# Block 0's y in three float32r passes, a one-operation mask, and a full-tile count, in the head of an attention and FFN layer

## The chip, the cores and the metric

One core of a Trainium2 chip runs the whole layer. The metric is the device time of one execution in microseconds (us). Engines: PE is TensorE (matmuls; PEld are its weight loads), DVE is VectorE, ACT is ScalarE, POOL is GpSimd, SP is SyncE, which issues most DMAs.

## The reference

Tokens x are (4, 2048, 256), taken as 8192 rows of 256 features. A first part is attention inside chunks of 32 tokens, a second part a feed-forward network with integer weights; each adds its input and ends in a layer norm.

```
Q, K, V = x @ W_q.T, x @ W_k.T, x @ W_v.T
mask[i, j] = decay ** (i - j) if i >= j else 0      # decay = sigmoid(log_decay[0]), 32 x 32
S = (Qc @ Kc.T) * mask                              # in each chunk of 32 tokens
O = S @ Vc
out = (sigmoid(x @ W_g.T) * O) @ W_o.T + x
x = layernorm(x + out)
h = silu(x @ (w_gate/127).T) * (x @ (w_up/127).T)   # 768 hidden features
x = layernorm(x + h @ (w_down/127).T)
```

## The kernel before

The tokens go in 16 blocks of 512 (TB). Everything is written out by hand, block by block; `in_turn` keeps the order of the written lines on each engine. While the FFN of block b runs, the attention of the next blocks runs between its pieces. The head, before that steady order, has to bring in and prepare the weights and to do the attention of blocks 0 and 1; it is what the change rearranges.

**Scores without Q and K.** The head makes m from W_q and W_k once (`make_m`, L220). For a block, y is m applied to x (feature-major, 256 x 512), and the scores are products of x and y in 32 x 32 pieces (`score_products`, L663, PE tiles of 128 x 32). `masked` (L679) multiplies the scores by the mask into sT on DVE. sT pairs two chunks: a row of 128 tokens has 64 columns, of which its own chunk's 32 are written; the other 32 stay zero from a memset at the start. `masked` therefore does four operations, one for each chunk of 32 partitions. `value_products` (L699, PE tiles of 64 x 64) multiplies sT and v into two PSUM banks po; L718 multiplies po by the gate into goT on DVE, for block 0 in four halves (`by_half`); `attn_residual` (L811) multiplies goT by W_o for block 0, the tile pa; L802 adds x and makes h.

**Two ways to multiply.** Block 0's gate (`attn_gate`, L587), value (`attn_v`, L629), y (`attn_y`, L608) and output (L811) are plain float32 matmuls; the profile shows each as two passes. All later blocks use `three` (L542): both operands are split into float32r parts and multiplied in three passes, high x high, low x low, gap x gap. Between the second and the third, ACT multiplies the PSUM bank by a constant (L542). `others()` runs the third pass later; the code calls it `g_rest`, `v_rest`, `y_rest` or `rest`.

**Making the parts.** Weights: `weight_parts` makes hi on ACT (L448) and lo on POOL (L449), `weight_up` scales lo on ACT (L455), `weight_gap` makes gap on POOL (L461). Tokens: hi on ACT (L472), lo on POOL (L476), gap on DVE (L481). Each is one operation of 128x512, two of them for a block's tokens.

**The order in the head** (L1078 on). Weight parts of wg; mask (`make_mask`, DVE); gate of block 0; hi and lo of block 1's tokens; value of block 0 with m made between its halves; y of block 0; gaps of wg and wv; parts of wo; gaps of block 1's tokens; gate and value of block 1 (first two passes); scores of block 0, then the load of block 2's xT, which takes the buffer of block 0's; rests of gate and value 1; y of block 1 (first two passes); values of block 0 (po); rest of y 1; output of block 0 (pa) with the scores of block 1 behind it; then block 2's value, and so on. `look_up` (L295, DVE) finds the largest integer of each FFN weight piece, `cast_...` (L286, ACT) turn the integers into the two FFN weight types. Whether any integer is too large is counted by a matmul of a [128, 1] tile of ones with a [128, 9] tile (`count_wide`, L313, the tile pw).

Of the kernel before, what the change touches and what calls it, by code (L numbers as in the profile page):

```python
# [47 lines left out]
F32 = mybir.dt.float32  # L48
# [4 lines left out]
ALU = mybir.AluOpType  # L53

P = 128
CHUNK = 32
PAIR = 2 * CHUNK
# [19 lines left out]
def kernel(  # L77
# [37 lines left out]
    def in_turn(ins):  # L115
        tc.keep_in_program_order(ins)

    def bank(name):
        return psum.tile([P, TB], F32, tag="ps", name=name)
# [119 lines left out]
        )  # L239
    chunk_mask = const.tile([P, CHUNK], F32, tag="chunk_mask", name="chunk_mask")  # L240
    nc.vector.tensor_scalar(chunk_mask, diff, 0.0, None, ALU.is_ge)
    table = tiny.tile([P, 1], F32, tag="table", name="table")
    in_turn(nc.scalar.activation(table, eps, AF.Sigmoid))
    bits = []
# [14 lines left out]
    def make_mask():  # L259
        in_turn(nc.scalar.activation(decay, decay, AF.Sigmoid))  # L260
        power = decay
        for i, (bit, factor) in enumerate(bits):
            in_turn(
                nc.vector.scalar_tensor_tensor(factor, bit, power, factor, ALU.mult, ALU.add)
            )
            in_turn(nc.vector.tensor_tensor(chunk_mask, chunk_mask, factor, ALU.mult))
            if i < len(bits) - 1:
                square = tiny.tile([P, 1], F32, tag=f"power_{i}", name=f"power_{i}")
                in_turn(nc.vector.tensor_tensor(square, power, power, ALU.mult))
                power = square  # L270

    sTs = [const.tile([P, NG, PAIR], F32, tag=f"sT_{i}", name=f"sT_{i}") for i in range(2)]
    for sT in sTs:
        nc.gpsimd.memset(sT, 0.0)

    def integers(w, w_int, name):

# [26 lines left out]
    def wide_counter():  # L304

        wide = const.tile([P, top.shape[1]], F32, tag="wide", name="wide")
        in_turn(nc.vector.tensor_scalar(wide, top, EXACT, None, ALU.is_gt))
        ones = tiny.tile([P, 1], F32, tag="ones", name="ones")
        nc.vector.memset(ones, 1.0)

        def count_wide():
            pw = bank("pw")[:1, : top.shape[1]]
            in_turn(nc.tensor.matmul(pw, lhsT=ones, rhs=wide, start=True, stop=True))  # L313
            count = tiny.tile([1, 1], F32, tag="count", name="count")
            in_turn(nc.vector.tensor_reduce(count, pw, mybir.AxisListType.X, ALU.add))
            return count

        return count_wide
# [123 lines left out]
    def weight_parts(w, name, tags):  # L442

        hi, lo = (
            const.tile([P, KD, D], F32R, tag=tag, name=f"{name}_{kind}")
            for tag, kind in zip(tags, ("hi", "lo"))
        )
        in_turn(nc.scalar.mul(hi, w, TOP))  # L448
        in_turn(nc.gpsimd.tensor_tensor(lo, w, hi.bitcast(F32), ALU.subtract))  # L449
        w_parts[name] = [hi, lo]  # L450

    def weight_up(name):

        lo = w_parts[name][1]
        in_turn(nc.scalar.mul(lo, lo.bitcast(F32), SHIFT))  # L455

    def weight_gap(name):

        hi, lo = w_parts[name]
        gap = const.tile([P, KD, D], F32R, tag=name, name=f"{name}_gap")  # L460
        in_turn(nc.gpsimd.tensor_tensor(gap, hi.bitcast(F32), lo.bitcast(F32), ALU.subtract))  # L461
        w_parts[name].append(gap)

    def pieces_of_tokens(t, name):

        hi, lo, gap = parts = [
            sums.tile([P, KD, TB], F32R, tag=f"{name[0]}_{kind}", name=f"{name}_{kind}")
            for kind in ("hi", "lo", "gap")
        ]

        def high(k):
            in_turn(nc.scalar.mul(hi[:, k, :], t[:, k, :], TOP))  # L472

        def low(k):
            whole = hi[:, k, :].bitcast(F32)
            in_turn(nc.gpsimd.tensor_tensor(lo[:, k, :], t[:, k, :], whole, ALU.subtract))  # L476

        def difference(k):
            whole = hi[:, k, :].bitcast(F32)
            in_turn(  # L480
                nc.vector.scalar_tensor_tensor(  # L481
                    gap[:, k, :], whole, -WHOLE, t[:, k, :], ALU.mult, ALU.add
                )
            )

        return parts, high, low, difference

    def token_parts(t, name):
        parts, high, low, difference = pieces_of_tokens(t, name)
        for k in range(KD):  # L490
            high(k)
            low(k)
        return parts, lambda: [difference(k) for k in range(KD)]
# [61 lines left out]
    def split_gate(b, x_parts):  # L555
        sg = work.tile([P, KD, TB], F32, tag="sg", name=f"sg_{b}")

        def finish(i, pb):
            in_turn(nc.scalar.activation(sg[:, i, :], pb, AF.Tanh, scale=HALF))

        return sg, three(f"g_{b}", feature_major(w_parts["wg"], x_parts), finish)
# [36 lines left out]

        return sg, gate

    def attn_y(b):

        xt = xTs[b]
        yT = work.tile([P, KD, TB], F32, tag="yT", name=f"yT_{b}")
        for fc in range(KD):
            py = bank(f"py_{b}_{fc}")
            for ec in range(KD):
                product = nc.tensor.matmul(  # L608
                    py,
                    lhsT=given["m"][:, ec, fc * P : (fc + 1) * P],  # L610
                    rhs=xt[:, ec, :],
                    start=(ec == 0),
                    stop=(ec == KD - 1),
                )
                in_turn(product)
            in_turn(nc.vector.tensor_copy(yT[:, fc, :], py))
        return yT

    def attn_v(b, between=None):
        xt = xTs[b]  # L620
        v = work.tile([P, NG, D], F32, tag="v", name=f"v_{b}")
        per = TB // D
        banks = []
        for h in range(NG // per):
            pv = bank(f"pv_{b}_{h}")
            for j in range(per):
                g = h * per + j
                for ec in range(KD):
                    product = nc.tensor.matmul(  # L629
                        pv[:, j * D : (j + 1) * D],  # L630
                        lhsT=xt[:, ec, g * P : (g + 1) * P],
                        rhs=given["wv"][:, ec, :],
                        start=(ec == 0),
                        stop=(ec == KD - 1),
                    )
                    in_turn(product)
            banks.append(pv)
            if h == 0 and between is not None:
                between()

        def copies():
            for h, pv in enumerate(banks):
                in_turn(nc.scalar.copy(flat(v, slice(h * per, (h + 1) * per)), pv))

        return v, copies
# [7 lines left out]
        masked(sTs[-1], ps, range(NG), in_steady_turn)  # L653
        return sTs[-1]

    chunks = [slice(i * CHUNK, (i + 1) * CHUNK) for i in range(P // CHUNK)]

    def score_products(ps, xt, yT, order):


# [12 lines left out]
    def masked(sT, ps, groups, order):  # L673


        for i, chunk in enumerate(chunks):
            at = i * CHUNK % PAIR
            order(
                nc.vector.tensor_tensor(  # L679
                    sT[chunk, groups.start : groups.stop, at : at + CHUNK],  # L680
                    ps[chunk],
                    chunk_mask[chunk, :].unsqueeze(1).to_broadcast([CHUNK, len(groups), CHUNK]),
                    ALU.mult,
                )
            )

    def by_pairs(t):
        return t.rearrange("p k (g r c) -> p (k g) r c", g=NG, c=PAIR)
# [386 lines left out]
        in_turn(nc.scalar.activation(table, eps, AF.Silu))  # L1075

    weight_parts(wg, "wg", ("wg_hi", "wg_lo"))
    make_mask()  # L1078
    back_to_silu()
    sg, gate = attn_gate(0)  # L1080
    gate()
    x_parts, x_gaps = token_parts(xTs[1], "x_1")

    def with_m():
        make_m()
# [1 line left out]
        weight_parts(wv, "wv", ("wv_hi", "wv_lo"))  # L1087
        weight_parts(m_sb, "m", ("wq", "wk"))

    v, copies = attn_v(0, with_m)  # L1090
    weight_up("wg")
    copies()
    weight_up("wv")
    yT = attn_y(0)
    weight_gap("wg")
    weight_gap("wv")
    in_turn(nc.scalar.mul(wo, wo, HALF**2))
    weight_parts(wo, "wo", ("wo_hi", "wo_lo"))
    x_gaps()
    sg_1, g_rest = split_gate(1, x_parts)  # L1100
    weight_up("m")
    weight_gap("m")
    fg, cast_fg = integers(ffn_gT, ffn_int[0], "fg")
    fu, cast_fu = integers(ffn_uT, ffn_int[1], "fu")
    fd, cast_fd = integers(ffn_dT, ffn_int[2], "fd")
    v_1, rest = split_v(1, x_parts)
    cast_fg(0)
    look_up([0])
    sT = attn_scores(0, yT)
    xTs[2] = load_xT(2)  # L1110
    g_rest()
    rest()
    look_up(range(1, 6))
    yT, rest = split_y(1, x_parts)
    goT = attn_values(0, sT, v, sg, by_half=True)
    cast_fg(1)
    rest()
    x_parts, x_gaps = token_parts(xTs[2], "x_2")
    cast_fu(0)

# [572 lines left out]
```

## Time and profile before

| What | us |
|---|---|
| median of three runs (from 483.99 to 485.03) | 484.53 |
| the profiled execution | 485.13 |
| its span, first to last instruction | 483.5 |
| PE busy in the span | 477.2 |
| POOL busy | 279.2 |
| start of the first matmul of block 0's gate | 4.41 |
| start of the FFN of block 0 on PE | 46.41 |

The granted TensorE clock is 0.997 of full speed over the span. A profile row gives start, duration, engine, line, operation, output and inputs with their shapes, and a count when like operations are merged. Matmul rows overlap, since a matmul ends some time after the next begins; what stands in brackets at the end of a row is how long the engine idled before it, and what ended that.

### The profile page before, as it was taken

The page shows a single profiled execution, that of the slowest core. Times are in us where ns is not written, and L with a number is a line of the kernel's source. Part 1 is how long each engine was busy: PE and PEld are TensorE (multiplying, and loading weights), DVE is VectorE, ACT ScalarE, POOL GpSimd, SP SyncE. Part 2 cuts the span into 40 slices and gives each one's busy share as a digit, 9 for nine tenths or more (in the row PEclk, how much of TensorE's full clock was granted, in tenths as well). Part 3 has the DMA queues.
Part 4 walks back from the last instruction along what each step waited for, and adds up shares of the span by engine and source line. Part 5 has one row for each costly group of instructions (what it writes and reads, how often), then busy time and mean ns, then how long its engine had stood idle before and what let it go on. Part 6 is the DMA issues. An engine that isn't in the chain of part 4 may idle for free.

```text
span 483.5 us, 12279 instructions
## 1 busy us (share of the span) xinstructions
PE 477.2 (99%) x4760; PEld 380.8 (79%) x4760; DVE 343.2 (71%) x795; ACT 370.3 (77%) x699; POOL 279.2 (58%) x285
## 2 busy tenths in 40 slices
PE   9999999999999999999999999999999999999995
PEld 5788787787978879697787978878697787968674
DVE  4587958776777766858676777866858676677656
ACT  4878788587877778788786887778788786786845
POOL 2835755655655566455655645565455555557764
PEclk9999999999999999999999999999999999999998
DMA  7730321221313114031321313114031211103102
GB/s 258 234 102 21 107 69 46 55 79 31 109 50 118 45 41 137 26 107 49 102 70 33 109 53 115 45 45 131 23 111 50 83 45 35 56 20 113 37 15 82
DMA packets 43323, 36.99 MB, mean 77 GB/s; under 512 B 4864, under 2 KB 39168, under 8 KB 43264
## 3 DMA queue, kind: packets, MB, share of 16 engines
q1 hardware_dynamic: 42144, 35.28, 23.3%
q10 hardware_dynamic: 1120, 0.92, 0.6%
q8 instruction: 38, 0.62, 0.5%
q14 instruction: 21, 0.17, 0.1%
HBM read 20.45 MB, written 8.39 MB: 60 GB/s over the span
## 4 chain that ended last, share of the span: by engine, by line
PE 98%; DMA 1%; DVE 0%; ACT 0%; issue 0%
PE fg L923 18%; PE fu L923 18%; PE fdn L764 13%; PE p_v L523 9%; PE p_y L501 9%; PE p_o L523 9%; PE p_g L501 9%; PE po L699 4%; PE ps L663 2%; PE fdn L1017 2%; PE fdn L1435 1%; PE fdn L745 1%; PE pg L587 1%; PE pa L811 1%; PE pv L629 1%; PE py L608 1%
## 5 line engine op out<-in xcount | busy, mean ns | idle before, releaser
L954 POOL TENSOR_TENSOR u_lo<-u,u_hi 128x512 f16<-128x512 f32 (+1 forms) x98 | 132.7, 1360 | 94.5 <-ACT u_hi L953 94.4
L948 DVE SCALAR_TENSOR_TENSOR u<-fu,s 128x512 f32<-128x512 f32 (+1 forms) x98 | 66.2, 675 | 76.4 <-ACT s L937 59.0
L953 ACT CAST u_hi<-u 128x512 fp32r<-128x512 f32 (+1 forms) x98 | 59.9, 611 | 36.0 <-DVE u L948 36.0
L937 ACT ACTIVATE s<-fg 128x512 f32<-128x512 f32 (+1 forms) x98 | 57.2, 584 | 15.4 <-PE fg L923 15.4
L923 PE MATMUL fg<-hT_hi,fg_hi 128*128 128x512 f32 (+1 forms) x196 | 67.5, 425 | 0.0
L923 PE MATMUL fu<-hT_hi,fu_hi 128*128 128x512 f32 (+1 forms) x196 | 60.2, 388 | 0.0
L923 PE MATMUL fg<-hT_lo,fg_lo 128*128 128x512 f16 (+1 forms) x196 | 58.0, 377 | 0.0
L923 PE MATMUL fu<-hT_lo,fu_lo 128*128 128x512 f16 (+1 forms) x196 | 57.4, 375 | 0.0
L476 POOL TENSOR_TENSOR go_lo<-goT,go_hi 128x512 fp32r<-128x512 f32 x30 | 39.3, 1331 | 14.4 <-ACT go_hi L472 14.4
L476 POOL TENSOR_TENSOR x_lo<-xT,x_hi 128x512 fp32r<-128x512 f32 x30 | 37.5, 1272 | 15.2 <-ACT x_hi L472 15.2
L481 DVE SCALAR_TENSOR_TENSOR go_gap<-go_hi,goT 128x512 fp32r<-128x512 f32 x30 | 45.0, 1540 | 0.8 <-ACT go_hi L472 0.7
L923 PEld LDWEIGHTS fg<-hT_hi,fg_hi 128*128 128x128 f32 x196 | 36.4, 189 | 9.9
L923 PEld LDWEIGHTS fu<-hT_hi,fu_hi 128*128 128x128 f32 x196 | 36.5, 188 | 8.1
L900 POOL TENSOR_TENSOR hT_lo<-hT,hT_hi 128x512 f16<-128x512 f32 x28 | 35.6, 1294 | 7.7 <-ACT hT_hi L899 7.6
L832 DVE TENSOR_TENSOR h<-p_o,x 128x512 f32<-128x512 f32 x30 | 19.3, 685 | 27.4 <-PE p_o L523 25.2
L923 PEld LDWEIGHTS <-fu_lo 128*128 128x128 f16 x196 | 19.2, 98 | 22.2
L764 PE MATMUL fdn<-fd_hi,u_hi 128*128 128x256 f32 x288 | 36.5, 276 | 0.0
L472 ACT ACTIVATE go_hi<-goT 128x512 fp32r<-128x512 f32 x30 | 17.3, 624 | 22.5 <-DVE goT L718 22.5
L764 PEld LDWEIGHTS fdn<-fd_hi,u_hi 128*128 128x128 f32 x288 | 34.4, 188 | 0.0
L764 PE MATMUL fdn<-fd_lo,u_lo 128*128 128x256 f16 x288 | 33.5, 273 | 0.0
L764 PEld LDWEIGHTS <-u_lo 128*128 128x128 f16 x288 | 27.2, 98 | 3.4
L923 PEld LDWEIGHTS <-fg_lo 128*128 128x128 f16 x196 | 15.0, 98 | 18.3 <-issue 9.4
(179 smaller groups left out, 1066.2 us busy)
## 6 DMA issues: line engine op xcount, KB each, us to landing
x<-in_x_dram SPq DMA_DIRECT2D x16, 512.0 KB, 3.8
xT<-in_xT_dram SPq DMA_DIRECT2D x15, 512.0 KB, 4.2
hT<-sq SPq DMA_DIRECT2D x224, 32.0 KB, 1.9
out_dram<-r SPq DMA_DIRECT2D x13, 512.0 KB, 3.1
out_dram<-r SPq DMA_DIRECT2D x7, 128.0 KB, 1.7
fg_int<-in_ffn_gT_dram SPq DMA_DIRECT2D x3, 256.0 KB, 7.2
fu_int<-in_ffn_uT_dram SPq DMA_DIRECT2D x3, 256.0 KB, 6.4
fd_int<-in_ffn_dT_dram SPq DMA_DIRECT2D x3, 256.0 KB, 5.5
```

Of the source, the lines that this page charges most:

```text
L476: in_turn(nc.gpsimd.tensor_tensor(lo[:, k, :], t[:, k, :], whole, ALU.subtract))
L481: nc.vector.scalar_tensor_tensor(gap[:, k, :], whole, -WHOLE, t[:, k, :], ALU.mult, ALU.add)
L501: nc.tensor.matmul(pb, lhsT=a[kind][:, k, i * P : (i + 1) * P], rhs=b[kind][:, k, :], start=kind + k == 0, stop=True, skip_group_check=True,)
L523: nc.tensor.matmul(pb[:, j * D : (j + 1) * D], lhsT=b[kind][:, k, g * P : (g + 1) * P], rhs=a[kind][:, k, :], start=kind + k + j == 0, sto ...
L699: product = nc.tensor.matmul(po[dims, dc * len(groups) + g, :], lhsT=v[rows, g, dc * P + dims.start : dc * P + dims.stop], rhs=sT[rows, g, :],
L764: nc.tensor.matmul(banks[g // per][:, g % per * D : (g % per + 1) * D], lhsT=part[:, g * P : (g + 1) * P], rhs=w, start=first and g % per ...
L900: nc.gpsimd.tensor_tensor(in_order[1], whole, in_order[0].bitcast(F32), ALU.subtract)
L923: product = nc.tensor.matmul(pb[:, part.start - cols.start : part.stop - cols.start], lhsT=w[kind][:, dc, hc * P : (hc + 1) * P], rhs=hT[k ...
L937: in_turn(nc.scalar.activation(s, pg, AF.Silu, scale=SCALE / H_UP))
L948: nc.vector.scalar_tensor_tensor(u, pu, U_UP / H_UP, s, ALU.mult, ALU.mult)
L953: in_steady_turn(nc.scalar.copy(hi, u))
L954: in_steady_turn(nc.gpsimd.tensor_tensor(lo, u, hi.bitcast(F32), ALU.subtract))
```

## The change

Three things change.

1. Block 0's y is made by `split_y`, as the other blocks' y is. For that block 0's tokens are split as well: hi on ACT and lo on DVE ahead of the mask, gap on DVE behind the mask, in buffers shared with `go_parts`. `attn_y` goes. The order around it changes: gate 1, value 1, y 0 in their first two passes, then the three rests, then y 1's first two passes, scores of block 0, load of block 2's xT, rest of y 1, values of block 0, output of block 0. The gaps of block 1's tokens move up to just behind the mask, m's gap ahead of wo's parts on POOL; wo's parts move behind the rests on ACT; the first look-up stays ahead of the values, look-ups 1 to 5 move behind goT.
2. `masked` multiplies by a mask of 64 columns that holds zeros beside each chunk, in one operation of all 128 partitions; sT needs no memset. This holds for all blocks.
3. The count's ones are a [128, 128] constant, and its result fills 128 partitions, of which one is used.

```diff
+    pair_mask = tiny.tile([P, PAIR // CHUNK, CHUNK], F32, tag="pair_mask", name="pair_mask")
+    nc.gpsimd.memset(pair_mask, 0.0)
...
+        for i, chunk in enumerate(chunks):
+            in_turn(nc.vector.tensor_copy(pair_mask[chunk, i % 2, :], chunk_mask[chunk, :]))
...
-    for sT in sTs:
-        nc.gpsimd.memset(sT, 0.0)
...
-            pw = bank("pw")[:1, : top.shape[1]]
+            pw = bank("pw")[:, : top.shape[1]]
+            ones = nc.const_aps.tensor(1.0, [P, P])
             in_turn(nc.tensor.matmul(pw, lhsT=ones, rhs=wide, start=True, stop=True))
...
-        for i, chunk in enumerate(chunks):
-            at = i * CHUNK % PAIR
-            order(
-                nc.vector.tensor_tensor(
-                    sT[chunk, groups.start : groups.stop, at : at + CHUNK],
-                    ps[chunk],
-                    chunk_mask[chunk, :].unsqueeze(1).to_broadcast([CHUNK, len(groups), CHUNK]),
-                    ALU.mult,
-                )
-            )
+        shape = [P, len(groups), PAIR // CHUNK, CHUNK]
+        order(
+            nc.vector.tensor_tensor(
+                sT[:, groups.start : groups.stop, :].rearrange("p g (h c) -> p g h c", c=CHUNK),
+                ps.unsqueeze(2).to_broadcast(shape),
+                pair_mask.unsqueeze(1).to_broadcast(shape),
+                ALU.mult,
+            )
+        )
...
     weight_parts(wg, "wg", ("wg_hi", "wg_lo"))
+    x_0, x_high, x_low, x_difference = pieces_of_tokens(xTs[0], "g_0")
+    for k in range(KD):
+        x_high(k)
+        x_low(k, nc.vector)
     make_mask()
     back_to_silu()
     sg, gate = attn_gate(0)
     gate()
     x_parts, x_gaps = token_parts(xTs[1], "x_1")
+    for k in range(KD):
+        x_difference(k)
+    x_gaps()
...
+    weight_up("wg")
     v, copies = attn_v(0, with_m)
-    weight_up("wg")
     copies()
     weight_up("wv")
-    yT = attn_y(0)
+    sg_1, g_rest = split_gate(1, x_parts)
+    weight_up("m")
     weight_gap("wg")
     weight_gap("wv")
+    weight_gap("m")
+    v_1, v_rest = split_v(1, x_parts)
+    yT, y_rest = split_y(0, x_0)
+    g_rest()
+    v_rest()
+    y_rest()
     in_turn(nc.scalar.mul(wo, wo, HALF**2))
     weight_parts(wo, "wo", ("wo_hi", "wo_lo"))
-    x_gaps()
-    sg_1, g_rest = split_gate(1, x_parts)
-    weight_up("m")
-    weight_gap("m")
...
-    v_1, rest = split_v(1, x_parts)
+    yT_1, y_rest = split_y(1, x_parts)
+    sT = attn_scores(0, yT)
+    yT = yT_1
+    xTs[2] = load_xT(2)
+    look_up(range(1))
+    y_rest()
     cast_fg(0)
-    look_up([0])
-    sT = attn_scores(0, yT)
-    xTs[2] = load_xT(2)
-    g_rest()
-    rest()
+    goT = attn_values(0, sT, v, sg, by_half=True)
     look_up(range(1, 6))
-    yT, rest = split_y(1, x_parts)
-    goT = attn_values(0, sT, v, sg, by_half=True)
     cast_fg(1)
-    rest()
```

More of the change, by code (lines that the diff above doesn't have):

```diff
@@ L241 @@
     nc.vector.tensor_scalar(chunk_mask, diff, 0.0, None, ALU.is_ge)
+    chunks = [slice(i * CHUNK, (i + 1) * CHUNK) for i in range(P // CHUNK)]
+    pair_mask = tiny.tile([P, PAIR // CHUNK, CHUNK], F32, tag="pair_mask", name="pair_mask")
+    nc.gpsimd.memset(pair_mask, 0.0)
     table = tiny.tile([P, 1], F32, tag="table", name="table")
@@ L307, in wide_counter @@
         in_turn(nc.vector.tensor_scalar(wide, top, EXACT, None, ALU.is_gt))
-        ones = tiny.tile([P, 1], F32, tag="ones", name="ones")
-        nc.vector.memset(ones, 1.0)
         def count_wide():
-            pw = bank("pw")[:1, : top.shape[1]]
+            pw = bank("pw")[:, : top.shape[1]]
+            ones = nc.const_aps.tensor(1.0, [P, P])
             in_turn(nc.tensor.matmul(pw, lhsT=ones, rhs=wide, start=True, stop=True))
             count = tiny.tile([1, 1], F32, tag="count", name="count")
-            in_turn(nc.vector.tensor_reduce(count, pw, mybir.AxisListType.X, ALU.add))
+            in_turn(nc.vector.tensor_reduce(count, pw[:1, :], mybir.AxisListType.X, ALU.add))
             return count
@@ L472, in high, with low @@
             in_turn(nc.scalar.mul(hi[:, k, :], t[:, k, :], TOP))
-        def low(k):
+        def low(k, eng=nc.gpsimd):
             whole = hi[:, k, :].bitcast(F32)
-            in_turn(nc.gpsimd.tensor_tensor(lo[:, k, :], t[:, k, :], whole, ALU.subtract))
+            in_turn(eng.tensor_tensor(lo[:, k, :], t[:, k, :], whole, ALU.subtract))
         def difference(k):
@@ L599, in attn_gate @@
         return sg, gate
[L601 to L613, printed above, removed]
-                )
-                in_turn(product)
-            in_turn(nc.vector.tensor_copy(yT[:, fc, :], py))
-        return yT
     def attn_v(b, between=None):
@@ L654, in attn_scores @@
         return sTs[-1]
-    chunks = [slice(i * CHUNK, (i + 1) * CHUNK) for i in range(P // CHUNK)]
     def score_products(ps, xt, yT, order):
```

## The prediction

> **What bounds the kernel now.** I read the page's chain first, then its busy shares, then the timelines of PE, POOL and DVE over the first 47 us, because the diff reaches the steady blocks in one place only (the mask product).
>
> ```profile
> PE 477.2 (99%) x4760; PEld 380.8 (79%) x4760; DVE 343.2 (71%) x795; ACT 370.3 (77%) x699; POOL 279.2 (58%) x285
> ...
> PE 98%; DMA 1%; DVE 0%; ACT 0%; issue 0%
> ```
>
> The first line is the busy times and shares, the second the chain by engine. The chain is PE for 98% of the span, and the waits of PE show a single one, 1.0 us at the start. So a microsecond of PE work taken from the head, or a hole put into it, should reach the end unchanged. The steady blocks repeat every 28.95 us with PE never idle; there the single mask product frees some 0.8 us of DVE a block (four operations 1.18 to 1.21 us, one of 128x256 about 0.42 like a goT piece), behind a PE that doesn't wait for it: I cost it at nothing.
>
> The head on PE, columns start, duration, engine, line, operation, count:
>
> ```profile
> 12.41 1.89 PE L629 MATMUL pv<-wv,xT 128*128 128x256 f32 x8
> 14.14 3.60 PE L608 MATMUL py<-xT,m_sb 128*128 128x512 f32 x8
> 17.17 1.03 PE L501 MATMUL p_g<-x_hi,wg_hi 128*128 128x512 f32 x2
> ...
> 25.40 0.62 PE L501 MATMUL p_y<-x_lo,m_lo 128*128 128x512 f32 x2
> 25.95 1.16 PE L699 MATMUL po<-sT,v 64*64 64x64 f32 x64
> 27.05 1.19 PE L501 MATMUL p_y<-x_gap,m_gap 128*128 128x512 f32 x4
> 28.08 3.61 PE L811 MATMUL pa<-wo,goT 128*128 128x256 f32 x16
> ```
>
> Rows overlap by a matmul's depth, so I go by ends (start plus duration): value 14.30, y of block 0 17.74, po 27.11, the rest of y 1 28.24, pa 31.69.
>
> POOL and DVE at the same time:
>
> ```profile
> 11.63 2.50 POOL L476 TENSOR_TENSOR x_lo<-xT,x_hi 128x512 fp32r<-128x512 f32 x2 [4.17 <-ACT x_hi L472]
> 14.11 1.26 POOL L449 TENSOR_TENSOR wv_lo<-wv,wv_hi 128x512 fp32r<-128x512 f32 x1
> 15.33 1.27 POOL L449 TENSOR_TENSOR m_lo<-m_sb,m_hi 128x512 fp32r<-128x512 f32 x1
> 16.56 1.27 POOL L461 TENSOR_TENSOR wg_gap<-wg_hi,wg_lo 128x512 fp32r<-128x512 f32 x1
> 17.79 1.29 POOL L461 TENSOR_TENSOR wv_gap<-wv_hi,wv_lo 128x512 fp32r<-128x512 f32 x1
> 19.04 1.74 POOL L449 TENSOR_TENSOR wo_lo<-wo,wo_hi 128x512 fp32r<-128x512 f32 x1
> 20.82 1.66 POOL L461 TENSOR_TENSOR m_gap<-m_hi,m_lo 128x512 fp32r<-128x512 f32 x1
> ```
>
> ```profile
> 18.38 2.95 DVE L481 SCALAR_TENSOR_TENSOR x_gap<-x_hi,xT 128x512 fp32r<-128x512 f32 x2
> ...
> 27.15 1.42 DVE L718 SCALAR_TENSOR_TENSOR goT<-sg,po 128x256 f32<-128x256 f32 x4 [0.64 <-PE po L699]
> ```
>
> The reader is to see two things. POOL works without a break from 11.63 to 22.48, and two of its operations are longer than 1.27 us exactly while DVE makes the two x_gap pieces, which alone take 0.68 each (the shortest of their 30) and here 2.95 together. The two alternate: the first x_gap piece gets on when wv_gap ends at 19.08, wo_lo then loses 0.47; the second gets on when wo_lo ends at 20.78 (20.78 + 0.55 = 21.33), and m_gap loses 0.39. Each x_gap piece among POOL's operations costs POOL some 0.44.
>
> **The change, part by part.**
>
> *y in three passes.* Removed: 8 passes, 17.74 - 14.30 = 3.44 us. Added: 12 passes of the kind of p_g, 8 of which end 1.85 us after py (19.59 - 17.74), so 0.231 each, 2.77. PE work falls by 0.67.
>
> *The po/pa order.* Before, the rest of y 1 (27.11 to 28.24) stands between po and pa. In the built order it stands ahead of po, and pa follows po at once. The rest costs 1.13 behind the 64x64 tiles where four passes are 0.92; the 0.21 then falls behind the scores instead, where gate's rest paid the same (23.25 - 22.12). Behind po it is gone: another -0.21.
>
> *POOL's queue.* The order is x_1_lo twice, wv_lo, m_lo, wg_gap, wv_gap, m_gap, seven operations, wo_lo behind them. That is 11.63 + 7 x 1.265 = 20.5 alone. But four gap pieces (two of x_0, new, and two of x_1, moved from 18.38) now stand on DVE right behind the mask, which ends at 11.4 plus four small copies (about 0.1 apart, like the bit operations), 11.85. Each takes one turn: x_1_lo to 14.57, wv_lo 16.27, m_lo 17.98, wg_gap 19.68, then wv_gap 20.95, m_gap 22.2.
>
> PE without waits: gate 1 to 16.15, value 1 to 17.99, y 0 to 19.83, the rests to 20.75, 21.67 and 22.59. The low pass of value 1 wants the scaled wv_lo at 16.45 and has it at 16.27 + 0.05 + 0.63 (ACT) = 16.95: a wait of 0.5. Behind that scaling ACT holds gate's two banks, m_lo (18.0 to 18.65, wanted as weights at 18.6) and value's two banks, ready at 19.6 and wanted from 21.3. The rest of y 0 loads m_gap as weights, some 0.36 ahead of the end of what precedes: at 21.3 without waits, and it is there at 22.25: together **0.95**, the 0.5 included. So bounds for POOL: nothing (no alternation, 20.5 is before 21.3) and 1.1 (a copy of the mask takes a turn as well); I take 0.95, from the two rows that show it.
>
> *The hole in front of pa.* Y 1 ends at 24.43 + 0.95 = 25.38; scores 0.69 (22.12 - 21.43), rest of y 1 1.13, po 1.09 (27.11 - 26.02): 28.29. goT waits for the whole of po (27.15 against 27.11), then two of its four pieces 0.35 apart, 0.42 long. DVE's queue up to there: the mask product 0.1 behind the scores (22.22 - 22.12), 0.36, one look-up 0.61, two yT copies 0.6 each: free at 28.35. goT's first half stands at 29.12; pa starts 0.16 later (load 0.04, matmul 0.12 behind the load, 27.96 to 28.08), at 29.28, and ends 3.61 later: **32.9 against 31.69, +1.2**. The hole is about 1.0 where before the rest of y 1 covered it, and without POOL's delay the sum would be +0.25.
>
> *Behind pa.* Five look-ups (0.6 each) now stand between goT and h, so h starts 4.36 behind goT, and the mask product of block 1 6.76 behind (30.86 to 33.26 is 2.40): it ends as the value passes of block 2 do, no wait, by 0.05. xT of block 2 is loaded behind the scores, 22.15 before, 26.1 now; its packets ended by 25.5, 3.4 later; so 29.5, two x_hi and two x_lo (3.2) end at 32.7, wanted at 34.3: hidden. Behind that load SP holds only the xT of block 3, which waits for block 1's scores anyway; ACT holds casts and wo_lo behind x_hi, wanted at p_o, 10 us later. p_o of block 1 waited 0.24 for go_lo (0.86 where its like take 0.64); POOL is then slightly ahead: -0.1. x_0's two x_hi and two x_lo lie in ACT's and DVE's idle time (6.1 to 8.35, 5.2 to 8.58): nothing; without that cover 0.6 each on the mask.
>
> *Count.* The row behind pw pays 0.21 (46.57 - 45.44 is 1.13 for eight passes of 0.92); a full tile should drop that, and two weight loads of 128 columns in place of one add about 0.12: -0.1. Bounds: -0.2 to +0.2. The two memsets of sT, and the smaller one that replaces them, lie on a POOL that idles from 2.9 to 6.20: nothing.
>
> Sum: +1.2 - 0.1 - 0.1 = **+1.0**. The profiled run took 485.13 (span 483.5 and 1.63 around it), 0.6 over the median of the runs shown, 484.53. I add to the median: **485.6**.
>
> The Trainium skill, GPSIMD Engine Reference, section Specifications, says that GpSimd shares its SBUF interfaces with VectorE and contends with DVE instructions with two SBUF inputs; the gap pieces are such, it gives no figure, and by the page alone the sum would lie anywhere from the +0.1 of no delay to the +1.0 here. The skill's TensorEngine Tiling (Array Packing), section Key Properties, says that changing the tiling mode drains TensorE; if that held on both sides of the count, the sum would be 0.2 lower, but the rows show the loss behind it only.
>
> **The rivals.**
>
> *No delay by POOL, not slower* (place: m_gap in front of the rest of y 0; decides when it is ready before 21.3). For: x_1_lo beside DVE operations with PSUM input kept 1.27. Against: wo_lo and m_gap above. Price: the 0.95 goes, +0.05, 484.6.
>
> *The look-ups become the wait.* They run beside x_lo on POOL; if they take turns too, the mask product of block 1 is up to 0.8 late and po of block 1 stands. Against: one look-up beside m_gap took 0.67, as alone. 486.4.
>
> *The lighter PE wins.* POOL free and goT covered after all (goT released by half of po): 0.67 + 0.21 + 0.1 come through, 483.5. Against: goT's row above.
>
> **How the numbers follow.** Forecast 0.5, POOL free 0.2, look-ups 0.2, lighter PE 0.1. A measurement of this kernel can tell about 0.2%, 1.0 us, from no change; the forecast lies on that line with some 0.4 either way, so of its half I count 0.3 as slower and 0.2 as the same; the look-ups are slower, POOL free the same (0.02 faster), the lighter PE faster (0.02 the same). Slower 0.50, same 0.40, faster 0.10. The range reaches from POOL free less the spread of the runs (0.5) to the look-ups: 484.0 to 486.4, with most of the lighter PE and some of the look-ups outside.
>
> **What would show it.** After: wv_lo's and m_lo's durations on POOL near 1.7; PE's loads idle on POOL in front of the rest of y 0 and on DVE (goT) in front of pa, about 1 us; pa's end at 32.9; py gone and p_y's passes 0.23 apart; the row behind pw back to 0.92. Wrong if m_gap ends before 21, if goT starts ahead of po's end, or if PE shows a new wait beyond 47 us.

## The result, and the profile after

The changed kernel takes **487.3 us** (median of six runs, 486.91 to 488.58), the kernel before beside it 484.84 (six runs, 483.99 to 485.24): a ratio of 1.0059 with a 95% interval from 1.0043 to 1.0075. It is 2.5 us slower. The prediction said 485.6 and a range to 486.4, so the direction held, and the size was two and a half times the forecast. The profiled execution took 487.46, its span is 485.9.

The busy times of the engines in the changed kernel, then two rows of the view of PE's waits (who waited for whom: us in total, times, longest):

```profile
PE 476.2 (98%) x4764; PEld 381.1 (78%) x4764; DVE 341.9 (70%) x754; ACT 373.6 (77%) x703; POOL 279.1 (57%) x284
...
PE p_g L504 <- DVE x_gap L484: 2.2, 2, 1.1
PE pa L793 <- DVE goT L700: 0.8, 1, 0.8
```

PE is busy for 1.0 us less than before and the span is 2.4 longer: PE now stands still, and DVE is what it waits for. Before, the same view had one row, the 1.0 us at the start. The timeline of PE in the head of the changed kernel (start, duration, engine, line, operation, output and inputs, count, and in brackets the idle time ahead of the row and what ended it):

```profile
11.55 1.89 PE L614 MATMUL pv<-wv,xT 128*128 128x256 f32 x8
...
20.79 0.47 PE L504 MATMUL p_g<-x_gap,wg_gap 128*128 128x512 f32 x1 [1.13 <-DVE x_gap L484]
22.38 0.96 PE L504 MATMUL p_g<-x_gap,wg_gap 128*128 128x512 f32 x3 [1.12 <-DVE x_gap L484]
...
28.78 1.16 PE L681 MATMUL po<-sT,v 64*64 64x64 f32 x64
30.78 3.72 PE L793 MATMUL pa<-wo,goT 128*128 128x256 f32 x16 [0.84 <-DVE goT L700]
```

There are two holes. The one in front of pa, 0.84 idle, was forecast. The other, twice 1.1 in front of the rest of gate 1, was not: PE waits there for the gap pieces of block 1's tokens, once for each. Why they are late, DVE's timeline shows:

```profile
11.55 3.95 DVE L276 COPY pair_mask<-chunk_mask 32x32 f32<-32x32 f32 x4
15.53 3.42 DVE L484 SCALAR_TENSOR_TENSOR g_gap<-g_hi,xT 128x512 fp32r<-128x512 f32 x2
18.88 3.44 DVE L484 SCALAR_TENSOR_TENSOR x_gap<-x_hi,xT 128x512 fp32r<-128x512 f32 x2
...
29.98 1.41 DVE L700 SCALAR_TENSOR_TENSOR goT<-sg,po 128x256 f32<-128x256 f32 x4
```

The four 32x32 copies of the mask, for which the prediction had 0.1 each, take 3.95 us together. One by one, in the view of the tile pair_mask (least, median and greatest duration in ns, then first and last start):

```profile
L276 DVE COPY pair_mask<-chunk_mask x4: 170/1238/1258, 11.6 to 14.3; 32x32 f32<-32x32 f32 x4
```

One takes 170 ns, the others 1.24 us and more. POOL at that time:

```profile
11.69 2.52 POOL L479 TENSOR_TENSOR x_lo<-xT,x_hi 128x512 fp32r<-128x512 f32 x2 [4.13 <-ACT x_hi L475]
14.15 1.30 POOL L452 TENSOR_TENSOR wv_lo<-wv,wv_hi 128x512 fp32r<-128x512 f32 x1
15.40 1.30 POOL L452 TENSOR_TENSOR m_lo<-m_sb,m_hi 128x512 fp32r<-128x512 f32 x1
16.65 1.76 POOL L464 TENSOR_TENSOR wg_gap<-wg_hi,wg_lo 128x512 fp32r<-128x512 f32 x1
18.37 1.73 POOL L464 TENSOR_TENSOR wv_gap<-wv_hi,wv_lo 128x512 fp32r<-128x512 f32 x1
20.06 1.71 POOL L464 TENSOR_TENSOR m_gap<-m_hi,m_lo 128x512 fp32r<-128x512 f32 x1
```

The first copy runs at 11.55, ahead of x_lo at 11.69. Each of the other three lasts as long as one of POOL's operations, and the last ends at 15.50, as wv_lo does (15.45). The gap pieces start four us late, and the last ends at 22.32 where the prediction's turns end them at about 18.4 (m_lo's end at 17.98 and some 0.44 more). POOL's own slow operations (1.7 in place of 1.3) are those beside the gap pieces; beside the copies wv_lo takes 1.30 and took 1.26 before, so the copies cost POOL next to nothing.

**Theory (turns):** while POOL works on SBUF, a DVE operation like these copies gets in only between two of POOL's operations, however small it is. So the number of DVE operations that meet POOL counts, not their size: three copies push the gap pieces back by three POOL operations. **First rival (slow copies):** a 32x32 copy is slow in itself. **Second rival (the order):** the copies stand beside the path, and the loss comes from the new order alone, as the prediction had it in front of pa.

### The profile page after: what moved, and what is told of

Read it like the earlier page. It is cut to its first block, busy times and chain, and to the rows that moved or that the text cites. A ratio compares the mean times of both kernels' runs of the same rounds, so it can differ in the third digit from the quotient of the medians.

```text
span 485.9 us, 12237 instructions
## 1 busy us (share of the span) xinstructions
PE 476.2 (98%) x4764; PEld 381.1 (78%) x4764; DVE 341.9 (70%) x754; ACT 373.6 (77%) x703; POOL 279.1 (57%) x284
## 4 chain that ended last, share of the span: by engine, by line
PE 87%; DVE 5%; ACT 2%; SPq 2%; issue 1%; DMA 1%; ACTq 0%; DVEq 0%
PE fg L905 17%; PE fu L905 16%; PE fdn L746 13%; PE p_o L526 8%; PE p_y L504 8%; PE p_v L526 8%; PE p_g L504 8%; PE po L681 3%; PE fdn L999 2%; PE ps L646 2%; SPq L864 2%; PE fdn L1425 1%; DVE x_gap L484 1%; DMA wg<-in_w_gT_dram 1%; PE pa L793 1%
## 5 line engine op out<-in xcount | busy, mean ns | idle before, releaser
L484 DVE SCALAR_TENSOR_TENSOR go_gap<-go_hi,goT 128x512 fp32r<-128x512 f32 x30 | 46.0, 1572 | 0.7 <-ACT go_hi L475 0.7
```

Source lines behind the costliest of these rows:

```text
L484: nc.vector.scalar_tensor_tensor(gap[:, k, :], whole, -WHOLE, t[:, k, :], ALU.mult, ALU.add)
```

## The experiments

Each ran in five rounds beside the kernel before on the same chip, whose median stands in brackets (e1, e2, e6 and e7 on one chip, e8, e9 and e10 on a second, e11 on a third, so across these groups the differences to the bracket count, not the times). The ratio is worked out from the runs themselves and can differ a little from that of the two medians. Because block 0's matmuls take a different time in each execution (last section), head times are compared where that doesn't matter, or are counted from the end of block 0's value.

### The copies later (e1_copies_late)

The changed kernel, with the four copies behind the rest of y 0.

```diff
+    def spread_mask():
         for i, chunk in enumerate(chunks):
             in_turn(nc.vector.tensor_copy(pair_mask[chunk, i % 2, :], chunk_mask[chunk, :]))
...
     y_rest()
+    spread_mask()
     in_turn(nc.scalar.mul(wo, wo, HALF**2))
```

> The changed kernel with one edit: the four copies that spread the mask into pairs stand behind y 0's rest on DVE instead of ahead of the gap pieces. Turns theory (a DVE operation on SBUF gets on only between two POOL operations, so each small copy costs a POOL operation's length, 1.25 us, while POOL is busy): the gap pieces start at 11.6 and end near 18.4 instead of 22.3, PE's two waits for x_gap (2.2 us) go, a wait of about 0.5 for wv_lo and 0.4 for m_gap come in their place; the copies take 0.1 to 0.2 us each where POOL is idle; pa ends at about 32.9 (34.5 in the changed kernel, 31.7 in the kernel before) and the time is 1.3 to 1.6 us under the changed kernel, 0.6 to 1.0 over the kernel before. Rival, slow copies (a copy of 32 partitions takes about 1 us wherever it stands): the copies still take 4 us, the mask product of block 0 is 2 us late, po waits, and the time is within 0.5 us of the changed kernel.

Measured 485.56 [484.92], ratio 1.0014 (1.0005 to 1.0023). Against the changed kernel some 2 us are gone: 1.8 by the differences to the kernel before (2.46 and 0.64), 2.2 by the ratios, and 1.6 by the ends of pa in the two profiles. The copies in their new place, in the view of the tile:

```profile
L277 DVE COPY pair_mask<-chunk_mask x4: 159/174/1236, 24.3 to 25.9; 32x32 f32<-32x32 f32 x4
```

Three take 0.17, and the one that meets wo_lo (on POOL from 24.59 to 25.88) takes 1.24. The same instruction is short without POOL and long beside it: slow copies are ruled out, and the turns hold here too. POOL:

```profile
11.61 3.19 POOL L480 TENSOR_TENSOR x_lo<-xT,x_hi 128x512 fp32r<-128x512 f32 x2 [4.14 <-ACT x_hi L476]
14.75 1.75 POOL L453 TENSOR_TENSOR wv_lo<-wv,wv_hi 128x512 fp32r<-128x512 f32 x1
16.46 1.73 POOL L453 TENSOR_TENSOR m_lo<-m_sb,m_hi 128x512 fp32r<-128x512 f32 x1
```

This is the picture that the prediction drew for the changed kernel: wv_lo and m_lo near 1.7, the gap pieces from 11.29 to 17.05, PE waiting for POOL (0.60 for x_lo, 0.46 for wv_lo) and 0.84 for goT, and pa ending at 32.87 where 32.9 was forecast. That the sum fits so closely is in part luck, since its parts don't: by the ends of the rows value 1's first passes come 0.41 later than was put (18.90 and 18.49), and the 0.45 forecast for m_gap falls away. So the copies are the one large thing that was mis-sized. The second rival falls as the only cause; the order has the 0.7 us that e1 still lies over the kernel before.

### One operation in place of four copies (e9_one_spread)

The changed kernel, with pair_mask made at the same place by one operation of 128x64: the mask times a tile of ones and zeros, which POOL sets at the start.

```diff
...
-        for i, chunk in enumerate(chunks):
-            in_turn(nc.vector.tensor_copy(pair_mask[chunk, i % 2, :], chunk_mask[chunk, :]))
+        in_turn(
+            nc.vector.tensor_tensor(
+                pair_mask,
+                chunk_mask.unsqueeze(1).to_broadcast([P, PAIR // CHUNK, CHUNK]),
+                pair_ones,
+                ALU.mult,
+            )
+        )
```

> The changed kernel with the four copies of 32 partitions replaced by one operation of 128x64 in the same place on DVE (the mask read twice, times a tile of zeros and ones that POOL fills at the start). It moves as many elements as two of the four copies would on 128 partitions. Turns theory (what costs is the number of operations that have to get between POOL's): the one operation gets in before POOL's x_lo or waits one turn, so the gap pieces end at 18.4 to 19.7 instead of 22.3, and the time is 1.3 to 1.9 us under the changed kernel, 0.5 to 1.2 over the kernel before. Rival (what costs is the work beside POOL, not the number of operations): the gap pieces end after 21 and the time is within 0.7 of the changed kernel.

Measured 485.74 [484.75], 1.0017 (1.0008 to 1.0025), like the copies moved away. DVE's timeline:

```profile
11.53 0.23 DVE L279 TENSOR_TENSOR pair_mask<-chunk_mask,pair_ones 128x64 f32<-128x64 f32 x1
```

It begins ahead of POOL's x_lo at 11.67 and takes 0.23 for twice the elements of all four copies; the gap pieces end at 17.43, earlier than the 18.4 to 19.7 expected. So four operations in that place cost what one doesn't. But this one never met POOL, so e9 alone doesn't tell number from work beside POOL. The copies themselves do, and the rows of e10 and e11 below: 32x32, 128x32 and 128x1 operations all take about 1.2 to 1.35 there.

### The mask and the count alone (e6_mask_count_alone)

The kernel before, with parts 2 and 3 of the change (the diff shown under the change, up to the multiply by `pair_mask`) and not part 1.

> The kernel before with the one-operation mask (and its four copies behind the mask, where nothing waits on DVE until 16.1) and the full-tile count, without y 0 in three passes and without any move. Turns theory: the copies take about 4 us here too, from 11.5 to 15.5, beside x_lo, wv_lo and m_lo, and cost nothing, since the first DVE operation behind them is y 0's copy at 16.1; the mask product falls from 1.2 us to 0.4, behind a PE that does not wait; the row behind the count loses 0.1. Time within 0.5 us of the kernel before, rather below. Rival, the steady blocks gain from the freed DVE: 1 us or more below the kernel before. Rival, the one-operation mask itself costs time: 1 us or more above.

Measured **484.28** [484.92], 0.9988 (0.9980 to 0.9997): a little faster than before, with the interval just under 1. The copies are as long here as in the changed kernel:

```profile
11.11 3.91 DVE L276 COPY pair_mask<-chunk_mask 32x32 f32<-32x32 f32 x4
```

But DVE's next operation, the copy of y, waits for PE until 15.46, and the copies end at 15.02. A stretched operation costs only what stands behind it: nothing in the old order, about two us in the new one, which put the gap pieces there. The count, in PE's timeline:

```profile
44.21 0.29 PE L316 MATMUL pw<-wide,const-float32-1.0 128*128 128x9 f32 x2
44.35 1.18 PE L526 MATMUL p_o<-wo_gap,go_gap 128*128 128x256 f32 x8
```

From the end of pw (44.50) to the end of the eight passes (45.53) are 1.03 where the kernel before took 1.13; the forecast -0.1 holds. The stall of p_o for go_lo (a row of 0.86 before) is 0.62 here. From the end of block 0's value to the FFN's first matmul it is 31.67 (13.70 to 45.37) against 32.11 before (14.30 to 46.41): the gain of some 0.4 lies wholly in the head, and the shorter mask product gives the steady blocks nothing, as was forecast.

### The y part alone (e7_y_alone)

The changed kernel, with the mask product of four operations, no copies, and the count of before (parts 2 and 3 undone).

> The changed kernel with the mask product of before (four operations, no copies) and the count of before: y 0 in three passes and all the moves alone. Turns theory: without the copies the gap pieces end near 18.4 and the wait for x_gap goes (-1.6); but the mask product of four operations ends 0.8 later, po waits for it some 0.3 and goT comes later on DVE, so the hole in front of pa grows: between 0.7 and 1.5 us under the changed kernel. Rival (the loss belongs to the new order of PE, whatever the mask): within 0.5 of the changed kernel.

Measured **488.23** [484.92], 1.0071 (1.0058 to 1.0084): 0.9 over the changed kernel by the medians (0.6 by the ratios), where I had expected it below. The gap pieces are on time (11.34 to 17.08) and PE doesn't wait for them. But the mask product takes its old length, and in the new order DVE is on PE's path. PE's timeline:

```profile
30.09 3.72 PE L794 MATMUL pa<-wo,goT 128*128 128x256 f32 x16 [1.46 <-DVE goT L701]
...
37.30 1.15 PE L682 MATMUL po<-sT,v 64*64 64x64 f32 x60 [0.39 <-DVE sT L662]
```

DVE's, for the first of these:

```profile
26.13 1.21 DVE L662 TENSOR_TENSOR sT<-ps,chunk_mask 32x128 f32<-32x128 f32 x4 [1.76 <-POOL wo_lo L452]
27.36 0.69 DVE L297 TENSOR_REDUCE top<-fg_int 128x1 f32<-128x512 int32 x1
28.08 1.29 DVE L570 COPY yT<-p_y 128x512 f32<-128x512 f32 x2
29.29 1.41 DVE L701 SCALAR_TENSOR_TENSOR goT<-sg,po 128x256 f32<-128x256 f32 x4
```

These rows lead to goT without a pause, and the mask product with 1.21 in place of 0.42 moves them all. The hole in front of pa grows to 1.46. Up to the end of pa e7 is still 0.69 ahead of the changed kernel (33.81 and 34.50), about what I had expected; it loses behind pa, where I hadn't looked: from there to the FFN's start it takes 15.28 against 14.13, 0.85 of the difference ahead of p_o, where block 1's values wait for the mask product as well, 0.19 in p_o's stall and 0.11 behind it, the count's. With the copies out of the way in both, e7 lies 2.7 over e1 (488.23 and 485.56). Of that 2.1 stand in the head (the FFN starts at 47.01 and 49.09), which is what the one-operation mask and the count are worth in this order by these two profiles. The rest, 0.3 behind the FFN's start and 0.3 to 0.4 outside the span (time less span is 1.9 to 2.0 in e7's runs and 1.5 to 1.7 in all others of these experiments), no run explains. I had taken parts 2 and 3 for small because they were so in the old order.

### The hole covered by y 1's rest (e2_cover)

The changed kernel, with y 0's rest first, value 1's rest between scores and values of block 0, y 1's rest behind the values, and m's gap first on POOL.

```diff
+    weight_gap("m")
     weight_gap("wg")
     weight_gap("wv")
-    weight_gap("m")
...
-    g_rest()
-    v_rest()
     y_rest()
+    g_rest()
...
     look_up(range(1))
-    y_rest()
+    v_rest()
     cast_fg(0)
     goT = attn_values(0, sT, v, sg, by_half=True)
+    y_rest()
```

> The changed kernel with the rests placed otherwise: y 0's rest first (m's gap first on POOL), gate 1's rest, y 1's first passes, scores 0, value 1's rest, po, y 1's rest, pa. The copies stay where they are. Hole theory (the 0.84 us in front of pa are a loss of their own, next to the late gap pieces): the hole goes, pa follows y 1's rest. Turns theory: x_0's gap pieces end at 19.0 and x_1's at 22.3 as before, so gate 1's rest still waits until 22.3, about 1.7 us, and then all follows; the time falls by about 0.8 to 1.3 us against the changed kernel, to 1.2 to 1.7 over the kernel before. If the hole were only a consequence of the late gap pieces, the time would not fall by more than 0.3.

Measured 485.52 [484.92], 1.0015 (1.0007 to 1.0024). The hole in front of pa is gone (po starts at 25.69, the rest of y 1 at 26.79, pa at 27.83 without a wait), and x_gap, though it ends at 21.11 behind the early copies, costs little, since gate's rest comes later. I had expected x_gap at 22.3 and a time 1.2 to 1.7 over the kernel before, and it is 0.6 over: POOL idled for 1.0 ahead of m_gap (16.57 to 17.59), and block 0's two gap pieces took 2.32 there instead of 3.42. But a new wait stands behind pa, in PE's timeline first, then DVE's:

```profile
35.23 1.16 PE L681 MATMUL po<-sT,v 64*64 64x64 f32 x64 [1.08 <-DVE sT L661]
...
28.22 1.28 DVE L570 COPY yT<-p_y 128x512 f32<-128x512 f32 x2
29.42 1.27 DVE L299 TENSOR_REDUCE top<-fg_int 128x1 f32<-128x512 int32 x2
```

The five look-ups (29.42 to 32.47 on DVE) stand ahead of h and of block 1's mask product. They take 0.6 each although POOL makes x_lo at that time, so it isn't by turns, as the prediction's rival had it, that they come out, but by their place in the queue. In the changed kernel y 1's two copies stand ahead of goT and the look-ups begin 1.33 behind goT's start (31.31 and 29.98); here y 1's rest, and with it the copies, comes behind the values, and they begin 2.53 behind it (29.42 and 26.89).

### The look-ups spread as well (e8_cover_lookups)

e2, with three look-ups ahead of block 0's scores, two ahead of its values and one behind y 1's copies.

```diff
+    look_up(range(3))
     sT = attn_scores(0, yT)
...
-    look_up(range(1))
+    look_up(range(3, 5))
     v_rest()
...
     y_rest()
-    look_up(range(1, 6))
+    look_up(range(5, 6))
```

> The kernel of e2 (rests placed otherwise) with the look-ups spread: three ahead of block 0's scores, two ahead of goT, one behind y 1's copies, instead of five behind goT. In e2 PE stands 1.08 us in front of po of block 1, for a mask product that DVE makes only after five look-ups, h and its moments. Look-up theory: that wait goes, the time falls by about 1.0 us against e2, to about 0.4 under the kernel before. Rival (something else, such as pa's end or h, sets that mask product): the wait stays above 0.5 and the time within 0.4 of e2.

Measured 484.54 [484.75], 0.9997 (0.9987 to 1.0007). The wait of 1.08 is gone, and with it 0.8 us by the differences to the kernel before (0.60 over it in e2, 0.21 under it here). With the look-ups out of that place in the queue nothing waits there.

### All of it moved (e10_all_moved)

e8, with the copies behind gate's rest and block 0's gap pieces ahead of the mask.

```diff
         x_low(k, nc.vector)
+    for k in range(KD):
+        x_difference(k)
     make_mask()
...
     g_rest()
+    spread_mask()
     in_turn(nc.scalar.mul(wo, wo, HALF**2))
```

> The kernel of e8 with the copies behind y 0's rest, and x_0's gap pieces ahead of the mask, where POOL is idle (from 7.5 to 11.6), instead of behind it. Turns theory: x_0's pieces take 0.65 each there; the mask then runs into POOL's x_lo, wv_lo and m_lo with its last six small operations, a turn each, without making POOL longer; x_1's gap pieces end at about 20.5, wanted at 20.8; x_lo, wv_lo and m_lo keep 1.27, so the waits of PE for them (0.6 and 0.5 in e1) go too. What is left is y 0's saving of 0.7 and 0.4 behind pa: 483.6 to 484.2 where the kernel before has 484.9, 0.3 to 0.7 under e8. Rival (the mask's small operations cost more turns than that): x_1's gap pieces end after 21.5 and the time is at or over e8's.

Measured **484.19** [484.75], 0.9990 (0.9981 to 0.9999). The y part now costs nothing, but it gains nothing over e6 either, though PE has 0.7 less to do. From the end of block 0's value to the FFN it is 31.76 (13.87 to 45.63), against 31.67 in e6. PE's small stops eat the gain: four passes of y 0's rest take 1.41 (19.67 to 21.08) in place of 0.92, in part for ACT's scaling, and value 1's first passes some 0.3 too much. And the mask itself still met POOL in this execution, in DVE's timeline:

```profile
11.82 1.23 DVE L267 SCALAR_TENSOR_TENSOR factor<-bit,power,factor 128x32 f32<-128x32 f32 x1
13.09 1.20 DVE L269 TENSOR_TENSOR chunk_mask<-chunk_mask,factor 128x32 f32<-128x32 f32 x1
14.21 3.52 DVE L485 SCALAR_TENSOR_TENSOR x_gap<-x_hi,xT 128x512 fp32r<-128x512 f32 x2
```

The last two operations of the mask are 0.25 and 0.19 a round earlier.

### Gate's rest ahead of y 0's (e11_gate_rest_first)

e10, with the rest of gate 1 ahead of that of y 0, and POOL's gaps in the order wg, m, wv, to take away the stop for ACT.

```diff
+    weight_gap("wg")
     weight_gap("m")
-    weight_gap("wg")
     weight_gap("wv")
...
-    y_rest()
     g_rest()
+    y_rest()
     spread_mask()
```

> The kernel of e10 with gate 1's rest between y 0's first passes and y 0's rest (and the gaps on POOL in the order wg, m, wv). In e10 y 0's rest follows its own first passes at once and stands 0.4 us for ACT, which has to multiply each bank in between; x_1's gap pieces are there at 17.7, so gate 1's rest can fill that time. Theory: the 0.4 goes and y 0's saving shows: about 1.0 us under the kernel before (0.9978 to 0.9984 of it). Rival (another wait, for wv_lo or m_gap, takes its place): within 0.3 us of e10, 0.6 under the kernel before.

Measured 485.87 [484.57], 1.0026 (1.0015 to 1.0037): 1.3 over the kernel before, and my expectation missed. DVE's timeline:

```profile
15.34 1.24 DVE L267 SCALAR_TENSOR_TENSOR factor<-bit,power,factor 128x32 f32<-128x32 f32 x1
16.61 1.22 DVE L269 TENSOR_TENSOR chunk_mask<-chunk_mask,factor 128x32 f32<-128x32 f32 x1
17.75 3.51 DVE L485 SCALAR_TENSOR_TENSOR x_gap<-x_hi,xT 128x512 fp32r<-128x512 f32 x2
```

In this execution POOL began 0.2 earlier than in e10's (11.52 and 11.72) and the mask stood 0.26 later, so that five of its operations met POOL and not two. Each took 1.2 to 1.35, a 128x1 product among them. x_gap came 3.5 later, gate's rest waited 1.3 for it, one pair copy met wo_lo, and the values of block 0 waited 1.26 for sT. So a shift of a quarter of a microsecond at 11.5 comes with a loss of 2.6 by the FFN's start, counted from the end of block 0's value (34.32 and 31.76). How much of it is the shift's and how much the order's is not shown: in e10 gate's rest comes behind y 0's and asks for x_gap over a microsecond later (20.91, in e11 19.55). This execution took 486.74, 0.9 over the median of e11's runs, which lie between 485.28 and 486.95, so the loss is not of this execution alone.

## Why the prediction was wrong, step by step

It went the way that was forecast, by a term that was mis-sized. Its steps up to the end of pa, by the ends of the rows of the two profiled executions:

| Step | Predicted | Measured |
|---|---|---|
| block 0's matmuls up to the end of its value | 0 | -0.86 |
| y 0 in three passes | -0.67 | -0.70 |
| waits in the first passes of gate 1 and value 1 (x_lo, wv_lo) | +0.5 | +0.7 |
| waits in the rests (gap pieces) | +0.45 | +2.76 |
| tile switch ahead of y 1's rest | -0.21 | -0.2 |
| order of po and pa | +1.16 | +1.11 |
| end of pa | +1.2 | +2.81 |
| from there to the FFN's start | -0.2 | -0.59 |

(Before, 31.69 and 46.41; after, 34.50 and 48.63. The 2.76 is 22.38 + 0.96 less the end of y 0's passes, 19.66, less the 0.92 that four passes take. It holds the 0.86 of the first row: POOL began no earlier for block 0's early matmuls (x_lo at 11.69, before at 11.63), so with the old start the wait would be about 1.9. Behind the FFN's start the spans differ by another 0.2.)

**The step that failed** is "plus four small copies (about 0.1 apart, like the bit operations), 11.85". They took 3.95 us, one at 0.17 and three at 1.24. The bit operations were the wrong row: they run from 2.35 to 5.21, where POOL does next to nothing (it idles from 2.90 to 6.20), and I knew in the same paragraph that POOL and DVE alternate. I gave the alternation to the large gap pieces only, with the bound "1.1 (a copy of the mask takes a turn as well)", which is one copy's turn, taken on POOL's side. But three took one, and a turn pushes DVE's own queue back by 1.24, while POOL loses nothing. So I looked for the harm on the wrong engine: not m_gap on POOL held PE up but x_gap on DVE, and gate's rest, for which the prediction had 19.83 without waits, began at 20.79 and went on at 22.38. e1 shows the size of the step: with the copies away pa ends at 32.87 and not at 34.50, and what is then left over against the forecast is small.

**POOL's turns for the gap pieces** held: 0.4 to 0.5 each, in the changed kernel on the operations four us further on. **The hole in front of pa** held (0.84 idle, 1.11 by ends); goT waits for the whole of po, as e2 shows best, where DVE is free (goT at 26.89, po's end at 26.85), so the rival of the lighter PE fell. **The look-ups** cost nothing in the changed kernel, as forecast (block 1's mask product ends at 37.06, its values start at 37.15), but with 0.1 to spare; e2, which put y 1's copies ahead of them, paid 1.08. The rival, that they take turns with POOL, did not show: they keep 0.6. **Behind pa** 0.59 came back where 0.2 was forecast: the count's 0.1 as it was put, the stall of p_o 0.28 (its four rows last 1.84 to the next, before 2.12) where I had counted 0.1, and 0.2 ahead of p_o, half of it in the row of block 1's values (1.09 to the next row, before 1.20). **The early gain** of 0.86 is not the change's (last section), and the wait for x_gap swallowed it.

**No delay by POOL**, the first rival, did not hold: in e1, where the copies are away, PE still waits 1.06, for x_lo and wv_lo. My 0.95 for it had the size but in part the wrong place, m_gap, which ends at 21.94 there and is wanted at 22.44, and that the sum came out right in e1 is luck to that extent.

What stays open: whether the 0.7 of PE work that y in three passes saves can be had at all. e10 comes to e6's time and not below, and e11, meant to take the rest, shows how narrow that order is. Also not explained are the two runs of the changed kernel at 488.51 and 488.58, against four from 486.91 to 487.46; that a mask operation more met POOL there would fit, and so would their lower granted clock (0.994 and 0.993, the other four 0.997 to 1.000), but only one execution has a trace. The best versions are e6 (0.9988) and e10 (0.9990); e6 is the simple one.

## What to carry to other kernels

The duration of a small operation is to be read from a row in which the other engine was as busy as it will be in the new place; beside a GpSimd that worked without a break, a small VectorE operation on SBUF (a copy or one with two inputs, not a look-up) cost here what one of GpSimd's costs, so count such operations, make one of four, or put them where GpSimd idles. Before moving work behind an operation, ask what stood behind it until now: a stretch that nobody waited for (e6) became two microseconds on the path (the changed kernel) with no change to itself. And parts of a change that look small in the old order must be priced again in the new: the mask and the count gave 0.4 in the head in the one and, with the copies out of the way, 2.1 in the other.

## What the runs showed of the hardware

**A turn is a whole instruction.** DVE operations on SBUF of 32x32, 128x32 and 128x1, between 0.15 and 0.25 alone, took 1.18 to 1.35 beside POOL operations of 128x512 with about 1.25 from start to start, in seven of the kernels. Larger ones took a turn too: two gap pieces 1.28 together with POOL idle (e10) and 3.4 to 3.5 beside it. Their effect on POOL differs: a gap piece adds 0.4 to 0.5 to one of its operations, a small one no more than 0.04 (wv_lo 1.30 and 1.26). Not affected were look-ups (reduction of one input, 0.67 beside m_gap before) and the copies of y out of PSUM (0.69 beside POOL's m_lo and wg_gap before, 0.69 in e10 beside wg_gap and wv_gap). The Trainium skill has the rule on the page SBUF — State Buffer, section Who interferes with whom: the pair of SBUF ports that VectorE shares with GpSimd is locked for a whole instruction by the one that starts first, and the other blocks; copies can be under it as well as operations with two SBUF inputs. The runs agree with it, with 1.24 for a copy of 0.17. Read for the copies, not only for the gap pieces, it would have put three of them at three POOL operations; the page does not say who is next when both engines have a queue, and here it was each in turn.

**A start that varies.** The first eight matmuls of block 0's gate, the same in all kernels, took 3.82 us in the changed kernel's profile, 4.71 in that of before and 5.04 in e7's; value 0 ended between 13.41 and 14.62. Where PE then waits for POOL the difference is lost: the values of block 0 start at 27.15 in e1 and at 27.09 in e7, whose value 0 ended 1.06 later, and e1's eleven runs lie within 0.42 us where the 29 of the kernel before beside it spread over 1.6. The Trainium skill, TensorE: Matmul & The Clock Gate, Part 1, says that TensorE starts on a slower clock and that how many matmuls it takes to leave it differs from run to run; a row of 3.82 to 5.04 for the same matmuls would fit, and so does the pace: the weight loads of these matmuls start 0.85 apart at first (5.43 and 6.28 before) and then 0.43 apart (6.82 and 7.25), and the kernels differ in how many are slow. But the granted clock in the records is 1.00 over the first 15 us of these three profiles, so no run here shows the clock as the cause.
